# One 512 KB store at the end of a kernel, issued as eight transfers of 96, 11, 6, 5, 4, 3, 2 and 1 rows

## The chip, the cores and the metric

The kernel runs on one core of one Trainium2 chip. The metric is the device time of one execution in microseconds (us), lower being better; times given for a kernel are medians of several runs on the same chip.

## The reference

128 samples `x[b]` of 128 channels by 1024 steps (float32) each get the product of their own subject's 128 x 128 weight matrix added. There are eight subjects, and an index says which one each sample has.

```python
def reference(x, subjects, weights):        # x (128,128,1024), subjects (128,), weights (8,128,128)
    w = weights[subjects]
    return x + jnp.einsum('bct,bcd->bdt', x, w)
```

64 MiB are read and 64 MiB are written; one sample is 512 KB, 128 rows of 4 KB.

## The kernel before

The samples are worked on in tiles of four (`NT` = 32 tiles, index `i`). A tile lies in one of `SLOTS` = 12 buffers `xs[k]`, 128 partitions (rows) by four samples of 1024 float32, so a row of one sample is 4 KB in one partition. SyncE (SP) issues the loads, one for each sample, on its own queue (q1 in the profile): 48 at once, and from then on a tile's four whenever the stores out of its buffer have landed. The eight weight matrices are loaded once, into `w_all`.

The work runs over pairs of samples (`j` from 0 to 63; tile `i`, samples `q0` to `q1` of the tile). GpSimd copies each sample's matrix out of `w_all` into one of four small buffers (L196), TensorE multiplies into one of two PSUM buffers (L206), VectorE adds the product to `x` in place (L217) and counts up `s_added`. ScalarE (ACT) does no arithmetic. It waits for `s_added` and issues the stores on its own queue (q10 in the profile), through the helper `transfer` (L57):

- each pair of the first tile by itself (1 MB),
- each whole tile from then on (2 MB, after its second pair),
- and of the last tile: the first pair (1 MB, samples 124 and 125), then sample 126 by itself (512 KB, 128 rows), then, behind a barrier, sample 127 by itself (L231, called `last` here).

Both queues are served by the core's 16 DMA engines. A DMA counts its semaphore up by 16 (`DMA`) in all, and each engine's part of it ends with a small write to that semaphore. The records of the trace show a 128-row store of one sample as 128 packets of 4096 B and 16 such writes of 4 B: eight rows and one write for each engine.

At the end SP waits for the stores of the last twelve tiles, one semaphore after another (L229, L230), and the end of the program waits for `last`. The first critical section ends with a barrier between ACT and SP; it stands between ACT's issue of sample 126 and its issue of `last`. SP's waits at L229 and L230 come after that barrier, and ACT does not wait for them.

The line that decides how sample 126 is stored is the argument `q1 - (b == B - 1)` of L223: for the last pair it takes one sample off, so that one 512 KB store goes out. Its landing is counted on `s_pair[...][1]` of the last tile, for which the last turn of the loop at L228 waits.

Of the kernel before, what the change touches and what calls it, by code (L numbers as in the profile page):

```python
# [30 lines left out]
G = 2  # L31
H = 2
# [3 lines left out]
SLOTS = 12  # L36
# [5 lines left out]
DMA = 16  # L42

IDLE = 3

ROWS = 4
QUEUES = {mybir.EngineType.SP: "qSPDynamicHW", mybir.EngineType.Activation: "qActDynamicHW"}
# [2 lines left out]
def transfer(nc, engine, out, in_):  # L50

    later, nc._always_lower_symbolic_ap = nc._always_lower_symbolic_ap, False
    ins, outs = engine.lower_ap_dma(in_), engine.lower_ap_dma(out)
    nc._always_lower_symbolic_ap = later
    return engine.add_instruction(  # L57
        mybir.InstDMACopy(
            name=nc.get_next_instruction_name(),
            engine=engine.engine,  # L60
            ins=ins,
            outs=outs,
            mode="Copy",
            cce_op=ALU.bypass,
            queue=QUEUES[engine.engine],
        )
    )


@with_exitstack  # L70
def kernel(
    ctx: ExitStack,
    tc: tile.TileContext,
    x: bass.AP,
    subjects: bass.AP,
    weights: bass.AP,
    out: bass.AP,
):
    nc = tc.nc
    B, C, T = x.shape  # L80
    S, _, D = weights.shape
    NT = B // (G * H)

    def sbuf(name, *shape, dtype=F32):
        return ctx.enter_context(nc.sbuf_tensor(name, list(shape), dtype)).ap()

    given, near, wrap, index = (
        sbuf(name, 1, B, dtype=I32) for name in ("given", "near", "wrap", "index")
    )
    w_all = sbuf("w_all", C, S, D)  # L90
    ws = [sbuf(f"w{i}", C, 1, D) for i in range(W_SLOTS)]
    zeros = sbuf("zeros", C, N)
    xs = [sbuf(f"x{i}", C, H * G, T) for i in range(SLOTS)]
    ps = [
        ctx.enter_context(nc.psum_tensor(f"ps{i}", [D, G, T], F32)).ap() for i in range(P_SLOTS)
    ]

    s_given = tc.alloc_semaphore("s_given")
    s_wall = tc.alloc_semaphore("s_wall")
    s_index = tc.alloc_semaphore("s_index")  # L100
    s_zeros = tc.alloc_semaphore("s_zeros")
    s_copied = tc.alloc_semaphore("s_copied")
    s_product = tc.alloc_semaphore("s_product")
    s_added = tc.alloc_semaphore("s_added")

    s_pair = [[tc.alloc_semaphore(f"s_pair{i}_{h}") for h in range(H)] for i in range(SLOTS)]


    s_first = tc.alloc_semaphore("s_first")

    def emptied(i, h):

        turns = i // SLOTS
        return (DMA * G + (DMA if h == H - 1 else 0)) * turns

    def loaded(i, q):

        h = q // G
        return s_pair[i % SLOTS][h], emptied(i, h) + DMA * G

    def load(engine, i, q):
        k, h = i % SLOTS, q // G
        transfer(
            nc,
            engine,
            xs[k][:, q, :],
            x[i * H * G + q].rearrange("(a r) t -> a (r t)", r=ROWS),
        ).then_inc(s_pair[k][h], DMA)

    def store(i, q0, q1):  # L130
        k, b = i % SLOTS, i * H * G
        transfer(
            nc,
            nc.scalar,
            out[b + q0 : b + q1].rearrange("g d t -> d g t"),
            xs[k][:, q0:q1, :].rearrange("d (o g) t -> d o (g t)", g=min(G, q1 - q0)),
        ).then_inc(s_first if i == 0 and q1 == G else s_pair[k][(q1 - 1) // G], DMA)

    with tc.tile_critical():  # L139

        nc.scalar.dma_start(given, subjects.rearrange("(o b) -> o b", o=1)).then_inc(s_given, DMA)

        nc.vector.memset(zeros, 0.0).then_inc(s_zeros, 1)  # L143
        nc.tensor.wait_ge(s_zeros, 1)
        for _ in range(IDLE):
            nc.tensor.matmul(  # L146
                ps[P_SLOTS - 1][:, G - 1, :N], zeros[:, :D], zeros, start=True, stop=True
            )

        nc.vector.wait_ge(s_given, DMA)
        nc.vector.tensor_scalar(near, given, -S, S - 1, ALU.max, ALU.min).then_inc(s_index, 1)  # L153
        nc.vector.wait_ge(s_index, 1)
        nc.vector.tensor_scalar(wrap, near, 0, S, ALU.is_lt, ALU.mult).then_inc(s_index, 1)  # L155
        nc.vector.wait_ge(s_index, 2)
        nc.vector.tensor_tensor(index, near, wrap, ALU.add).then_inc(s_index, 1)  # L157
        nc.gpsimd.wait_ge(s_index, 3)


        nc.sync.dma_start(w_all, weights.rearrange("s c d -> c s d")).then_inc(s_wall, DMA)  # L161
        for i in range(NT):
            k = i % SLOTS
            if i == SLOTS:
                nc.sync.wait_ge(s_first, DMA)
            if i >= SLOTS:
                nc.sync.wait_ge(s_pair[k][H - 1], emptied(i, H - 1))
            for q in range(H * G):
                load(nc.sync, i, q)


        for j in range(NT * H):
            i, q0, q1 = j // H, j % H * G, (j % H + 1) * G
            k = i % SLOTS
            p = ps[j % P_SLOTS]

            ahead = j < P_SLOTS
            if ahead:  # L180
                nc.tensor.wait_ge(*loaded(i, q0))
            for q in range(q0, q1):
                b = i * H * G + q
                if b % R == 0:
                    _, subject = nc.values_load_multi_w_load_instructions(
                        index[0:1, b : b + R],
                        engines=[mybir.EngineType.Pool],
                        min_val=0,
                        max_val=S - 1,
                        skip_runtime_bounds_check_because="the index is clamped on the chip above",  # L190
                    )
                if b == 0:
                    nc.gpsimd.wait_ge(s_wall, DMA)
                if not ahead and q == q0:
                    nc.gpsimd.wait_ge(s_added, j - P_SLOTS + 1)
                copy = nc.gpsimd.tensor_copy(  # L196
                    ws[b % W_SLOTS], w_all[:, bass.ds(subject[b % R], 1), :]
                )
                if not ahead and q == q0:
                    copy.wait_op(*loaded(i, q0), "sem-ge")  # L200
            copy.then_inc(s_copied, 1)

            nc.tensor.wait_ge(s_copied, j + 1)
            for q in range(q0, q1):
                for t in range(0, T, N):
                    mm = nc.tensor.matmul(  # L206
                        p[:, q % G, t : t + N],
                        ws[(i * H * G + q) % W_SLOTS][:, 0, :],
                        xs[k][:, q, t : t + N],
                        start=True,  # L210
                        stop=True,
                    )
            mm.then_inc(s_product, 1)

            mine = xs[k][:, q0:q1, :]
            nc.vector.wait_ge(s_product, j + 1)
            nc.vector.tensor_tensor(  # L217
                mine, p, mine, ALU.add
            ).then_inc(s_added, 1)

            if i == 0 or q1 == H * G or i == NT - 1:
                nc.scalar.wait_ge(s_added, j + 1)
                store(i, q0 if i in (0, NT - 1) else 0, q1 - (b == B - 1))  # L223

    with tc.tile_critical() as waits:
        for i in range(NT - SLOTS, NT):  # L228
            nc.sync.wait_ge(s_pair[i % SLOTS][H - 1], emptied(i + SLOTS, H - 1))  # L229
        nc.sync.wait_ge(s_pair[(NT - 1) % SLOTS][0], emptied(NT - 1 + SLOTS, 0) + DMA)  # L230
    last = nc.scalar.dma_start(out[B - 1], xs[(NT - 1) % SLOTS][:, H * G - 1, :])  # L231

    tc.add_manual_dep(
        last.ins,
        waits.name,
        mybir.DependencyInfo(mybir.DependencyClass.NoSync, mybir.DependencyReason.SCHED_ONLY),
        reason="the end of the program waits for it",
    )
# [27 lines left out]
```

## Time and profile before

| what | value |
|---|---|
| device time, median of 3 runs | 326.48 us (326.29 to 326.70) |
| span of the profiled execution (first to last of the program's own instructions) | 325.4 us |
| median less that span | 1.1 us |
| TensorE / VectorE busy | 74% / 45% of the span |
| end of the last VectorE add | 278.7 us |
| DMA traffic | 134.85 MB, mean 414 GB/s |
| ACT begins to issue sample 126 | 300.46 us |
| ACT issues `last` | 305.02 us |
| the landings of `last` on its semaphore, first / median / last of 16 | 320.64 / 321.3 / 324.42 us |

The page has one profiled execution; the three runs are executions of the same program, and the profiled one has no device time of its own on the page, only its span. In what follows the 1.1 us that the median has over the span are taken as what lies around it. All times inside the execution count from the span's start. The DMA share of a stretch is the mean over 16 engines: 1.00 means that all were at work, 0.06 that one was. A row of the timeline that reads "ACTq" is the time for which ACT was held by issuing a DMA; the transfer itself goes on afterwards.

### The profile page before, as it was taken

What the parts mean: (1) busy time and instruction counts of PE and PEld (TensorE: products, weight loads), DVE (VectorE), ACT (ScalarE), POOL (GpSimd) and SP (SyncE); (2) the same over time, 40 slices, a digit from 0 to 9 for tenths busy, and PEclk for the clock granted to TensorE, in tenths of its full rate; (3) what the DMA queues carried; (4) which work ended last, traced back from release to release, by engine and by line L of the source; (5) the groups of instructions that cost most, each with busy time, mean ns of one, the idle gap of its engine ahead of it and who ended that gap; (6) DMA issues with size and microseconds to landing.
All of it is one profiled execution on the core that took longest, in us unless ns stands there. A gap on an engine that the chain in (4) does not pass through costs nothing.

```text
span 325.4 us, 1606 instructions
## 1 busy us (share of the span) xinstructions
PE 241.1 (74%) x518; PEld 95.2 (29%) x518; DVE 147.9 (45%) x68; POOL 34.3 (11%) x132
## 2 busy tenths in 40 slices
PE   6999988988888888888888888888888689000000
PEld 2444332333333333333333333333333233000000
DVE  1375754555555555454555555554554544200000
POOL 1011111011111111111011111111111010000000
PEclk9999999999999999999999999999999889655555
DMA  6999999999999999999999999999999999999994
GB/s 250 413 418 421 428 425 422 420 428 427 426 421 427 429 415 427 424 431 423 423 435 417 416 432 424 428 417 428 433 419 424 418 437 415 429 425 427 426 428 201
DMA packets 16074, 134.85 MB, mean 414 GB/s; under 512 B 2625, under 2 KB 3650, under 8 KB 3906
## 3 DMA queue, kind: packets, MB, share of 16 engines
q1 hardware_dynamic: 7184, 67.64, 49.7%
q10 hardware_dynamic: 8882, 67.11, 49.1%
q8 instruction: 4, 0.07, 0.1%
q14 instruction: 4, 0.03, 0.0%
HBM read 67.63 MB, written 67.11 MB: 414 GB/s over the span
## 4 chain that ended last, share of the span: by engine, by line
PE 42%; DVE 20%; issue 16%; POOL 4%; DMA 2%; POOLq 1%; SPq 0%
PE ps L206 42%; DVE x L217 20%; POOL w L196 4%; DMA x<-in_x_dram 2%; POOLq L196 1%; SPq L57 0%; SPq L161 0%; POOLq L139 0%; SPq L262 0%; SPq L139 0%
## 5 line engine op out<-in xcount | busy, mean ns | idle before, releaser
L206 PE MATMUL ps<-x,w 128*128 128x512 f32 x512 | 236.1, 607 | 33.6 <-POOL w L196 32.1
L217 DVE TENSOR_TENSOR x<-ps,x 128x2048 f32<-128x2048 f32 x64 | 146.7, 2292 | 129.1 <-PE ps L206 129.1
L206 PEld LDWEIGHTS ps<-x,w 128*128 128x128 f32 x512 | 93.3, 191 | 176.6 <-issue 93.9
L196 POOL COPY w<-w_all 128x128 f32 x128 | 34.1, 296 | 238.0 <-DMA x<-in_x_dram 207.7
L146 PE MATMUL ps<-zeros 128*128 128x512 f32 x6 | 5.0, 992 | 1.7 <-DVE zeros L143 1.7
L146 PEld LDWEIGHTS ps<-zeros 128*128 128x128 f32 x6 | 1.8, 328 | 3.7 <-issue 2.1
L143 DVE MEMSET zeros<- 128x512 f32 x1 | 0.5, 485 | 1.1 <-SPq L139 1.1
L153 DVE TENSOR_SCALAR near<-given 1x128 int32<-1x128 int32 x1 | 0.2, 215 | 0.6 <-DMA given<-in_itok_B_dram 0.6
L157 DVE CUSTOM_DVE_ANT_0 index<-near,wrap 1x256 uint16<-1x256 uint16 x1 | 0.3, 278 | 0.0
L155 DVE TENSOR_SCALAR wrap<-near 1x128 int32<-1x128 int32 x1 | 0.2, 216 | 0.0
L253 POOL MEMSET const-float32-0.0<- 128x1 f32 x1 | 0.1, 99 | 0.2 <-issue 0.2
L253 POOL MEMSET const-bfloat16-1.0<- 128x1 bf16 x1 | 0.1, 102 | 0.0
L253 POOL MEMSET const-uint8-127<- 128x1 uint8 x1 | 0.1, 102 | 0.0
L253 POOL MEMSET const-float32-1.0<- 128x1 f32 x1 | 0.1, 99 | 0.0
## 6 DMA issues: line engine op xcount, KB each, us to landing
x<-in_x_dram SPq DMA_DIRECT2D x128, 512.0 KB, 32.3
out_dram<-x ACTq DMA_DIRECT2D x30, 2048.0 KB, 47.3
out_dram<-x ACTq DMA_DIRECT2D x3, 1024.0 KB, 13.9
out_dram<-x ACTq DMA_DIRECT2D x2, 512.0 KB, 21.1
w_all<-in_L_cond_weights_dram SPq DMA_DIRECT2D x1, 512.0 KB, 4.5
given<-in_itok_B_dram ACTq DMA_DIRECT2D x1, 0.5 KB
```

The lines of the kernel that those rows point to most:

```text
L143: nc.vector.memset(zeros, 0.0).then_inc(s_zeros, 1)
L146: nc.tensor.matmul(ps[P_SLOTS - 1][:, G - 1, :N], zeros[:, :D], zeros, start=True, stop=True)
L153: nc.vector.tensor_scalar(near, given, -S, S - 1, ALU.max, ALU.min).then_inc(s_index, 1)
L155: nc.vector.tensor_scalar(wrap, near, 0, S, ALU.is_lt, ALU.mult).then_inc(s_index, 1)
L157: nc.vector.tensor_tensor(index, near, wrap, ALU.add).then_inc(s_index, 1)
L196: copy = nc.gpsimd.tensor_copy(ws[b % W_SLOTS], w_all[:, bass.ds(subject[b % R], 1), :])
L206: mm = nc.tensor.matmul(p[:, q % G, t : t + N], ws[(i * H * G + q) % W_SLOTS][:, 0, :], xs[k][:, q, t : t + N], start=True, stop=True,)
L217: nc.vector.tensor_tensor(mine, p, mine, ALU.add).then_inc(s_added, 1)
L253: nc = _bacc.Bacc("TRN2", target_bir_lowering=False, num_devices=1)
```

## The change

The store of sample 126 becomes eight stores, of rows 0 to 95, 96 to 106, 107 to 112, 113 to 117, 118 to 121, 122 to 124, 125 to 126, and 127. They are issued by ACT one after another, in this order and on the same queue, and count a semaphore of their own, `s_shares`, up to 128. The wait of SP for the last tile's second pair becomes a wait for `s_shares`. The store of samples 124 and 125 before it and `last` behind it are as they were.

```diff
+SHARES = 96, 11, 6, 5, 4, 3, 2, 1
...
+    s_shares = tc.alloc_semaphore("s_shares")
...
+    def store_rows(i, q, d0, d1):
+        return transfer(
+            nc,
+            nc.scalar,
+            out[i * H * G + q, d0:d1],
+            xs[i % SLOTS][d0:d1, q, :],
+        )
...
             if i == 0 or q1 == H * G or i == NT - 1:
                 nc.scalar.wait_ge(s_added, j + 1)
-                store(i, q0 if i in (0, NT - 1) else 0, q1 - (b == B - 1))
+                if b < B - 1:
+                    store(i, q0 if i in (0, NT - 1) else 0, q1)
+                else:
+                    d = 0
+                    for rows in SHARES:
+                        store_rows(i, q0, d, d + rows).then_inc(s_shares, DMA)
+                        d += rows
...
     with tc.tile_critical() as waits:
-        for i in range(NT - SLOTS, NT):
+        for i in range(NT - SLOTS, NT - 1):
             nc.sync.wait_ge(s_pair[i % SLOTS][H - 1], emptied(i + SLOTS, H - 1))
+        nc.sync.wait_ge(s_shares, DMA * len(SHARES))
         nc.sync.wait_ge(s_pair[(NT - 1) % SLOTS][0], emptied(NT - 1 + SLOTS, 0) + DMA)
     last = nc.scalar.dma_start(out[B - 1], xs[(NT - 1) % SLOTS][:, H * G - 1, :])
```

## The prediction, made before the change was run

> **What bounds the kernel now.** I read the page first: the row of DMA shares, the bytes under it and the two queues.
>
> ```profile
> DMA  6999999999999999999999999999999999999994
> GB/s 250 413 418 421 428 425 422 420 428 427 426 421 427 429 415 427 424 431 423 423 435 417 416 432 424 428 417 428 433 419 424 418 437 415 429 425 427 426 428 201
> ...
> q1 hardware_dynamic: 7184, 67.64, 49.7%
> q10 hardware_dynamic: 8882, 67.11, 49.1%
> ```
>
> The DMA engines are full from the second slice to the last but one, at 415 to 435 GB/s; only the first and the last slice (8.1 us each) fall off. The page's chain of waits follows TensorE and VectorE; the last add ends at 278.7 us, and the 47 us behind it are the stores' backlog. So the kernel is as long as its DMA traffic, and the change, which moves no byte more or less, can only act on the fall-off at the end. I therefore cut the end into short windows.
>
> ```profile
> core 0: us, PE busy (x) PEld busy (x) DVE busy (x) POOL busy (x), PEclk, DMA share, GB/s
> ...
> 319.50:320.00 0.50, 0.00 (x0) 0.00 (x0) 0.00 (x0) 0.00 (x0) 0.50 1.00 410
> 320.00:320.40 0.40, 0.00 (x0) 0.00 (x0) 0.00 (x0) 0.00 (x0) 0.50 0.95 389
> 320.40:320.80 0.40, 0.00 (x0) 0.00 (x0) 0.00 (x0) 0.00 (x0) 0.50 0.73 297
> 320.80:321.20 0.40, 0.00 (x0) 0.00 (x0) 0.00 (x0) 0.00 (x0) 0.50 0.50 205
> ...
> 321.60:322.00 0.40, 0.00 (x0) 0.00 (x0) 0.00 (x0) 0.00 (x0) 0.50 0.23 92
> 322.00:322.40 0.40, 0.00 (x0) 0.00 (x0) 0.00 (x0) 0.00 (x0) 0.50 0.05 20
> ...
> 323.60:324.00 0.40, 0.00 (x0) 0.00 (x0) 0.00 (x0) 0.00 (x0) 0.50 0.05 20
> 324.00:324.40 0.40, 0.00 (x0) 0.00 (x0) 0.00 (x0) 0.00 (x0) 0.50 0.00 0
> ```
>
> The last column but one is the share of 16 engines at work: all until 320, half at 321, and from 322.2 to 324.0 a share of 0.05 to 0.08, which is one engine. That one engine is the end of the kernel. The landing records of `last` say the same: counted from the first of the 16, nine engines are done within 0.75 us, six more between 1.39 and 1.91 us, and one at 3.78 us. I call it the late engine. It is late by the same 3.7 to 3.8 us at every store that lands after 271 us, so it only has to work off the queue that it has; which of the 16 it is, no record tells.
>
> Last, ACT's issues (start, time held) and SP's waits.
>
> ```profile
> 300.46 4.01 ACTq L57 DMA_DIRECT2D out_dram<-x  x1
> 305.02 0.54 ACTq L231 DMA_DIRECT2D out_dram<-x  x1
> ```
>
> ```profile
> SPq L139 <- ACTq L139: 26.1, 1, 26.1
> SPq L229 <- DMA out_dram<-x: 18.0, 3, 9.5
> ```
>
> ACT is held 4.01 us over sample 126, because the queue's rings are full, and 0.54 us over `last`, when there was room. Both are issued 13 us before the first engine comes to them.
>
> **The change part by part.** *What an engine pays for a row.* In the lone engine's stretch the eight 4096 B packets of `last` start 155 to 156 ns apart, and a semaphore write is followed 6 ns later by the next packet. With all engines at work the step is the same, so a row costs the engine that carries it 0.155 us, whatever the others do, and a further semaphore write 0.006 us.
>
> *Where the rows go.* Before, each engine has eight rows of sample 126. The load of the index, a single row, shows one data packet and one semaphore write by an engine: a transfer of one row occupies one engine. I take it (an assumption; the trace has no transfer of 2 to 15 rows) that 96 rows give six to each of 16 engines, and that a transfer of n rows below 16 gives one row each to n engines, counted from the same first engine every time. By place in that count the rows are 13, 12, 11, 10, 9, 8, five times 7 and five times 6, together 128. [...]
>
> *What that is worth.* If the late engine stands at place 12 to 16, it loses two rows: 2 x 0.155 = 0.31 us less. At places 7 to 11 it loses one and gets one more semaphore write: 0.15 less. At place 6: +0.01. At places 5, 4, 3, 2, 1: +0.17, +0.33, +0.50, +0.66 and +0.82 (five rows and seven writes). No other engine takes over the end: the next lands 1.87 us before the late one, and 0.82 more still leaves it 1.05 us ahead. So the most that the change can bring by its rows is 0.31 us, 0.1% of the time, and about 0.2% (0.65 us) is what a measurement of this kernel can tell from no change.
>
> *ACT.* One issue becomes eight. The first (six rows and a write for each engine instead of eight) is held by full rings as the one before, about 4 us. The other seven cost between 0.54 us (the issue of `last`) and 0.62 us (the longest of the first twelve, with room in the rings), 4.0 to 4.5 us together with the gaps; I take 4.2, as these rows are the same instruction. Behind them stand the barrier and `last`, which moves from 305.0 to about 309.3 us. The cover is the backlog: the first engine reaches sample 126 at 317.8 us, the late one at 321.5. So this costs nothing. Uncovered it would cost its 4.2 us.
>
> [...]
>
> *SP.* One wait changes its semaphore; nothing is queued behind it but the other waits of the end. In before, SP is through these 0.47 us ahead of the landing of `last`, and the shares land ahead of `last` on every engine as sample 126 did, so it stays hidden.
>
> *Sum.* The mean over places 6 to 16 is (0.01 - 5 x 0.15 - 5 x 0.31) / 11 = -0.21 us. On the profiled execution: span 325.4 - 0.2 = 325.2, with 1.1 around it 326.3, against a median of 326.48.
>
> [...]
>
> **The rivals.**
>
> *R1, the late engine is given more rows.* The place is sample 126's part of its ring; the price 0.17 to 0.82 us; it decides from place 5 down, and passes 0.65 us at places 2 and 1. For it: nothing in the trace ties lateness to a place, and five of 16 places have it. Against: 11 places do not. Time 326.7 to 327.3.
>
> *R2, ACT is held at each of the eight.* The 512 KB store was held 4.01 us and the 1 MB store before it 4.5, hardly less than 2 MB stores (4.7), so holding isn't in proportion to size. Eight times 4.0 would put `last` at some 333 us; the quickest landing of any of the helper's transfers took 5.2 us, so the end would come 13 us or more later: about 340. It decides from 2.6 us an issue (the 21 us to the late engine's arrival, divided by eight). Against it: `last` found room at once, and SP's queue held 15 to 16 transfers.
>
> *R3, the late engine is late by another amount.* Stores that land from 162 to 233 us show it 2.5 to 3.3 us behind, the one at 252 us 7.5, those after 271 us 3.7 to 3.8. The jump falls where the loads run thin. With other timing it may not come back the same: 0.5 to 1.2 us less, or as much more. Against: the three runs lie within 0.41 us. Time 325.3 to 326.0, seldom 327.
>
> *R4, the split isn't what it says.* If each small transfer goes to a single engine, that engine has 6 + 32 = 38 rows, 30 x 0.155 = 4.7 us more: 327.4 on one of the first engines (they are 3.78 us ahead), 331.2 on the late one. For it: the only small transfer of the trace used one engine. Against: it had only one row.
>
> **How the numbers follow.** Forecast (places 6 to 16): 0.48, all within 0.2%. R1: 0.25, of which 0.13 is within and 0.12 slower. R2: 0.05, slower. R3: 0.14, of which 0.12 faster, 0.02 slower. R4: 0.08, slower. Together faster 0.12, same 0.61, slower 0.27. The range is from 325.8 (the nearer half of R3) to 327.4 (the whole of R1 and measurement noise); outside lie R2, R4 and the far half of R3, under 0.2. The forecast's own range is 326.1 to 326.6.
>
> **What would show it.** In the profile of the changed kernel the packets of 4096 B stay 256 and the writes of 4 B on q10 become 561 - 16 + 48 = 593 (16+11+6+5+4+3+2+1 = 48). The landing counts of `s_shares` show the split. The last engine's packets between its last 8192 B packet and `last` number six, seven or eight if the forecast holds, nine to 13 under R1. Eight ACT issues stand between 300.5 and 309 us, seven of them near 0.6; holds of 4 us would be R2. Windows at the end should show one engine for about 1.5 to 1.9 us; a much shorter or longer stretch is R3. The forecast is wrong if the time leaves 326.1 to 326.6, and its mechanism if the late engine's rows don't fall.

## The result and the profile after

The changed kernel takes 328.17 us (median of 3, 328.05 to 328.42) against 326.48: 1.69 us more, ratio 1.0052, 95% interval 1.0032 to 1.0071. The forecast was 326.3, a little under the time before, in a range up to 327.4. The time is outside the range, and the kernel became slower where it was to become faster.

The page says that the body of the kernel is as it was; only the last two slices of the DMA rows have moved (before: 428 and 201 GB/s at the end).

```profile
DMA  7999999999999999999999999999999999999993
GB/s 253 414 418 427 428 420 427 423 424 425 426 430 423 426 424 425 419 428 429 426 424 422 424 427 423 426 427 425 425 424 423 428 423 427 425 429 425 429 422 144
DMA packets 16106, 134.85 MB, mean 413 GB/s; under 512 B 2657, under 2 KB 3682, under 8 KB 3938
```

The same bytes move in 32 packets more: the 48 - 16 semaphore writes that the prediction counted. The end in short windows:

```profile
320.00:320.40 0.40, 0.00 (x0) 0.00 (x0) 0.00 (x0) 0.00 (x0) 0.50 0.93 277
320.40:320.80 0.40, 0.00 (x0) 0.00 (x0) 0.00 (x0) 0.00 (x0) 0.50 0.51 205
320.80:321.20 0.40, 0.00 (x0) 0.00 (x0) 0.00 (x0) 0.00 (x0) 0.50 0.50 184
...
321.60:322.00 0.40, 0.00 (x0) 0.00 (x0) 0.00 (x0) 0.00 (x0) 0.50 0.45 133
322.00:322.40 0.40, 0.00 (x0) 0.00 (x0) 0.00 (x0) 0.00 (x0) 0.50 0.18 72
...
324.40:324.80 0.40, 0.00 (x0) 0.00 (x0) 0.00 (x0) 0.00 (x0) 0.50 0.07 31
324.80:325.20 0.40, 0.00 (x0) 0.00 (x0) 0.00 (x0) 0.00 (x0) 0.50 0.03 10
```

Read the last two columns together. Before, a share of 0.95 came with 389 GB/s and one of 0.50 with 205: 25.6 GB/s for each engine at work. After, 0.93 comes with 277 and 0.45 with 133, that is 18.5 GB/s an engine; the windows between them are less slow (0.51 with 205 is 25.1, 0.50 with 184 is 23.0). So in some windows the engines are not fewer, they are slower while at work: a busy share says that an engine has a packet in hand, not at what pace it moves. Then comes the stretch of one engine, now up to 325.

The packet records show where. In the kernel before, from 290 us on, none of the 256 packets of 4096 B (159 ns) and of the 8192 B ones (309 or 311 ns) is longer than that. After the change 21 are, by 5.35 us in all, and all of them start once the first engines have reached the eight transfers. The late engine's row packets of sample 126 take, in ns:

```
96-row transfer: 300, 295, 951, 380, 159, 159 | 11 rows: 159 | 6 rows: 159 | 5 rows: 159 | then eight of last, 159 each
```

ACT's issues, start and time held:

```profile
299.60 4.00 ACTq L59 DMA_DIRECT2D out_dram<-x  x1
...
303.63 0.94 ACTq L59 DMA_DIRECT2D out_dram<-x  x1
...
309.07 0.84 ACTq L59 DMA_DIRECT2D out_dram<-x  x1
...
310.56 0.39 ACTq L249 DMA_DIRECT2D out_dram<-x  x1
```

`last` is issued at 310.6 us and its first landing is at 320.6: the cover held.

**A measure of the end.** The landing records allow a finer measure than the time of a run. Stage A is the time from the last of the 16 landings of the last 2 MB store to the last landing of samples 124 and 125, B from there to the last landing of sample 126, C from there to that of `last`. In before it is 2.47, 1.23 and 1.26 us, 4.96 in all; after the change 2.68, 2.91 and 1.14, 6.73 in all, 1.77 us more, where the medians differ by 1.69. (The two spans differ by 1.0 only: the profiled execution of before was a long one, its landing of that 2 MB store 0.74 us later. Executions whose span and time are both known lie 1.7 to 1.85 us apart, so that span of 325.4 belongs to a time of about 327.1, not 326.5.) This sum follows the medians through all the kernels run, mostly within 0.2 us and at most 0.4, though it comes from one execution and they from several:

| kernel | how sample 126 is stored | A, B, C (us) | sum, less before | median less before (us) | ratio, 95% interval | packets too long, us in all |
|---|---|---|---|---|---|---|
| before | 128 rows | 2.47, 1.23, 1.26 | | | | 0, 0 |
| after | 96, 11, 6, 5, 4, 3, 2, 1 | 2.68, 2.91, 1.14 | +1.77 | +1.69 | 1.0052 (1.0032 to 1.0071) | 21, 5.35 |
| e1 | 96, 32 | 3.25, 1.30, 1.24 | +0.82 | +1.10 | 1.0034 (1.0021 to 1.0046) | 7, 1.50 |
| e2 | 8 x 128 rows of 512 B | 2.58, 1.59, 1.05 | +0.26 | +0.35 | 1.0012 (1.0003 to 1.0021) | 5, 0.05 |
| e3 | 8 x 16 rows | 3.74, 1.60, 0.98 | +1.35 | +1.33 | 1.0040 (1.0027 to 1.0053) | 27, 7.31 |
| e4 | as after, from DRAM | 2.87, 1.57, 1.14 | +0.61 | +0.58 | 1.0019 (1.0010 to 1.0028) | 4, 0.77 |
| e5 | 8 x 16, spread in DRAM | 3.85, 1.61, 0.96 | +1.45 | +1.84 | 1.0055 (1.0042 to 1.0068) | 26, 5.27 |
| e6 | 128 rows, 12 KB apart in DRAM | 2.46, 1.24, 1.26 | 0.00 | +0.13 | 1.0002 (0.9993 to 1.0011) | 0, 0 |
| e7 | 96, 8 x 4 | 3.99, 0.98, 1.25 | +1.25 | +1.28 | 1.0037 (1.0024 to 1.0050) | 37, 7.80 |
| e8 | 8 x 16, to scratch | 3.20, 1.76, 1.12 | +1.12 | +1.15 | 1.0036 (1.0023 to 1.0049) | 35, 6.63 |
| e9 | 16 from 0, 20, 64, 80, 96, 112 | 2.52, 1.18, 1.03 | -0.24 | -0.24 | 0.9991 (0.9982 to 0.9999) | 15, 2.51 |
| e10 | 16 from 16, 48, 64, 80, 96, 112 | 2.55, 1.18, 1.08 | -0.16 | -0.25 | 0.9995 (0.9985 to 1.0005) | 12, 3.11 |
| e11 | 16 from 0, 16, 48, 64, 80, 96, 112 | 3.66, 1.40, 0.99 | +1.09 | +1.34 | 1.0033 (1.0016 to 1.0050) | 21, 5.31 |
| e12 | 16 from 0, 32, 64, 80, 96, 112 | 2.55, 1.19, 1.01 | -0.22 | -0.18 | 0.9996 (0.9987 to 1.0004) | 18, 3.49 |
| e13 | rows 0 to 15, eight times | 2.54, 2.26, 1.28 | +1.11 | +1.10 | 1.0034 (1.0022 to 1.0046) | 89, 30.3 |
| e14 | rows 16 to 31, eight times | 3.58, 2.41, 1.28 | +2.32 | +2.36 | 1.0075 (1.0062 to 1.0089) | 115, 46.2 |
| e15 | rows 32 to 47, eight times | 2.53, 2.64, 1.23 | +1.44 | +1.32 | 1.0038 (1.0024 to 1.0052) | 104, 33.9 |
| e16 | rows 48 to 63, eight times | 4.09, 1.98, 1.23 | +2.34 | +2.53 | 1.0078 (1.0064 to 1.0092) | 116, 48.1 |
| e17 | e10 again | 2.94, 1.20, 1.04 | +0.21 | +0.27 | 1.0007 (0.9999 to 1.0016) | 14, 3.56 |
| e18 | e10 with 16 and 48 last | 3.19, 1.19, 1.04 | +0.46 | +0.50 | 1.0012 (1.0003 to 1.0021) | 12, 2.79 |

Stages are of one profiled execution each; medians are of 3 to 12 executions beside the kernel before on the same chip. "Too long" is over 165 ns for 4096 B and 317 ns for 8192 B.

### The profile page after: what moved, and what is told of

The parts are those of the page before. It is cut to its first block, busy times and chain, and to the rows that moved or that the text cites. A ratio compares the mean times of both kernels' runs of the same rounds, so it can differ in the third digit from the quotient of the medians.

```text
span 326.4 us, 1613 instructions
## 1 busy us (share of the span) xinstructions
PE 240.5 (74%) x518; PEld 95.3 (29%) x518; DVE 147.9 (45%) x68; POOL 34.3 (11%) x132
## 4 chain that ended last, share of the span: by engine, by line
PE 42%; DVE 20%; issue 16%; POOL 4%; DMA 2%; POOLq 1%; SPq 0%
PE ps L217 42%; DVE x L228 20%; POOL w L207 4%; DMA x<-in_x_dram 2%; POOLq L207 1%; SPq L59 0%; SPq L172 0%; POOLq L150 0%; SPq L280 0%; SPq L150 0%
```

## The experiments

### What lengthens the packets: e1 to e4

Three theories stood: A, the rows that an engine reads; B, the number of transfers and semaphore writes; C, nothing but the late engine's nine rows.

e1_96_32, the change without its seven small transfers:

```diff
-SHARES = 96, 11, 6, 5, 4, 3, 2, 1
+SHARES = 96, 32
```

> Sample 126 in two transfers, 96 and 32 rows (six and two rows for each of 16 engines): the change without its seven small transfers, rows even again. In the changed kernel the records show 21 packets of the end that take longer than in the kernel before (4096 B: 294 to 951 ns instead of 159), 5.35 us too much in all, 1.36 us of it on the late engine's part of the 96 rows. Theory A (which engine reads which partitions: in a 96-row transfer an engine reads six neighbouring rows, others than in a 128-row one, and gets into the way of engines that read the same partitions): long packets stay, 0.5 to 1.4 us over the kernel before. Theory B (the many small transfers and their semaphore writes make the packets long): no long packets, within 0.2 us of before. Theory C (only the number of rows of the late engine counts, nine in the changed kernel): no long packets, within 0.1 us of before.

Measured: +1.10 us with two transfers and eight rows for every engine. C and B fall: the rows are even, there is one transfer more than before, and still seven packets are too long; stage A alone is 0.78 us longer. How long the late engine is held in stage A differs much from profile to profile: with the same 96-row transfer first it takes 2.68 us in the changed kernel, 3.25 here and 3.99 in e7.

e2_cols, as many transfers as the change, but each of all 128 rows:

```diff
-SHARES = 96, 11, 6, 5, 4, 3, 2, 1
+SHARES = (128,) * 8
...
-            out[i * H * G + q, d0:d1],
-            xs[i % SLOTS][d0:d1, q, :],
+            out[i * H * G + q, :, d0:d1],
+            xs[i % SLOTS][:, q, d0:d1],
```

> Sample 126 in eight transfers of all 128 rows by 128 columns each (512 B a packet): as many transfers and more semaphore writes than the change, but every engine keeps the rows that it has in the kernel before. Theory A: no packets that wait; 0.1 to 0.4 us over before, for 64 packets of 512 B at 22 to 27 ns instead of eight at 155. Theory B: as the changed kernel or worse, 1.4 to 1.7 us over. Theory C: as A.

Measured: +0.35 us, and no packet more than 15 ns too long. B falls a second time. Stage B is 0.36 us longer, and smaller packets account for most of it: on the late engine packets of 512 B start 23.5 ns apart, so 64 of them and eight writes take 0.30 us more than eight of 4096 B and one write. Stages A and C differ by +0.11 and -0.21 us.

e3_8x16, even rows again, but 16 neighbours at a time:

```diff
-SHARES = 96, 11, 6, 5, 4, 3, 2, 1
+SHARES = (16,) * 8
```

> Sample 126 in eight transfers of 16 rows: one row for each engine in each, so eight rows for every engine as before, but all 16 engines read 16 neighbouring partitions at a time. Theory A: more and longer packets than in the changed kernel, over 5 us too much in all, and an end 1 to 3 us over before. Theory B: as the changed kernel, 1.4 to 1.7 us over, as there are as many transfers. Theory C: 0.04 us over before (seven more semaphore writes).

Measured: +1.33 us, 27 packets, 7.31 us. The prices of A are met. e2 has eight transfers too; it differs in the rows that a transfer reads, but also in the size of its packets. e13 to e16 below change the rows alone.

e4_dram, the change's split without reading SBUF:

```diff
-            xs[i % SLOTS][d0:d1, q, :],
+            x[i * H * G + q, d0:d1],
```

> The changed kernel, but the eight transfers of sample 126 take the input x of that sample in DRAM as their source instead of the sum in SBUF (this sample's product is left out of the output): the same split over engines, the same writes to DRAM, no reading of SBUF partitions. Theory A, with the collision on the side of SBUF: no long packets among the rest, and an end up to 0.3 us over before (the late engine's ninth row). With the collision on the side of the writes to DRAM: as the changed kernel, 1.4 to 1.7 us over. Theory B: as the changed kernel. A copy from DRAM to DRAM may have a pace of its own, which the late engine's rows would show when it is alone.

Measured: +0.58 us, 4 packets too long, 0.77 us; the late engine's nine rows take 159 ns each again. So most of the loss goes with the reading of SBUF. I had expected none, though: three 8192 B packets are held (392, 512 and 606 ns), and stage A is 0.40 us too long. What holds them when no transfer of sample 126 reads SBUF stays open.

### SBUF or DRAM: e5, e6, e8, and a place check, e7

e5_sbuf_only and its control e8_scratch write to a scratch tensor, 16 KB apart or row after row (e5 is shown; the comment, added here, has e8's line):

```diff
+    scratch = nc.dram_tensor("scratch", (512, T), F32).ap()
...
-SHARES = 96, 11, 6, 5, 4, 3, 2, 1
+SHARES = (16,) * 8
...
+        rows = scratch.rearrange("(g e r) t -> g e r t", e=16, r=4)
-            out[i * H * G + q, d0:d1],
+            rows[d0 // 16, :, 0],          # e8_scratch: scratch[d0:d1]
```

> [...] Theory A-SBUF (engines collide where they read the same partitions): long packets as in e3_8x16, some 7 us too much in all, and 0.8 to 1.9 us over before. Theory A-DRAM (they collide where they write to neighbouring places in DRAM): hardly any, within 0.3 us of before.

> The control of e5_sbuf_only: eight transfers of 16 rows, written to the scratch tensor row after row, as e3_8x16 writes them to the output (output of sample 126 left out). Both theories: as e3_8x16, 1.0 to 1.6 us over before, with some 7 us too much in long packets.

e6_dram_only keeps the 128-row store and spreads its rows in DRAM:

```diff
-SHARES = 96, 11, 6, 5, 4, 3, 2, 1
+SHARES = (128,)
...
+        rows = scratch[: 3 * 128].rearrange("(p r) t -> p r t", r=3)
-            out[i * H * G + q, d0:d1],
+            rows[:, 0],
```

> One transfer of 128 rows for sample 126, as in the kernel before on the side of SBUF, but written to a scratch tensor with its rows 12 KB apart, so that each engine writes to other places modulo 128 KB than it does elsewhere (output of sample 126 left out). A-SBUF: no long packets, within 0.2 us of before. A-DRAM: long packets, 0.5 us or more over before.

Measured: e5 +1.84 us with 26 packets too long, e8 +1.15 with 35, e6 +0.13 (its interval takes in no change) with none, and stages as in before to 0.01 us. Changing the places in DRAM made no long packet, changing the rows read in SBUF did: A on the side of SBUF. That e5 lies above e8, with fewer packets too long (5.27 us in all, where some 7 were expected), was not foreseen and stays open.

e7_96_4s:

```diff
-SHARES = 96, 11, 6, 5, 4, 3, 2, 1
+SHARES = (96,) + (4,) * 8
```

> The changed kernel with other shares: 96 rows and then eight transfers of four rows, so that four engines get 14 rows and the other twelve six. In the changed kernel the late engine had nine rows and four writes, which is place 5 of the count; here it should have six rows and one write, if its place is the engine's and not chance. Rows alone (theory C): 0.3 us under before. Theory A: the 96 rows collide as in e1_96_32, 0.5 to 1.1 us over before, and less than the changed kernel. Should the late engine have 14 rows, the place is not fixed.

Measured: the late engine has six rows and one write, as its place 5 in the changed kernel asks (any place from 5 on would do), so stage B is 0.98 us, 0.25 less than before, close to the 0.31 of two rows. But stage A is 3.99 us (three of the late engine's 8192 B packets took 555, 388 and 865 ns), and the whole +1.28 us. The saving by rows is real and is lost several times over.

### Whose rows: e9 to e18

The records name no row and no engine for a packet, so these runs vary the rows that are read. e9 to e18 store sample 126 in transfers of 16 rows from given first rows, some rows left out of the output or stored several times (e9 is shown, with a comment added here):

```diff
-SHARES = 96, 11, 6, 5, 4, 3, 2, 1
+SHARES = 0, 20, 64, 80, 96, 112        # e9; the first rows of the others are in the table
...
-                    d = 0
-                    for rows in SHARES:
-                        store_rows(i, q0, d, d + rows).then_inc(s_shares, DMA)
-                        d += rows
+                    for d in SHARES:
+                        store_rows(i, q0, d, d + 16).then_inc(s_shares, DMA)
```

> Which partitions must be read for the late engine to be held? Sample 126 in six transfers of 16 rows (0, 20, 64, 80, 96 and 112 onward; the other 32 rows of that sample are left out of the output), so six rows for each engine. [...] Time between 0.3 us under before (two rows less) and 0.7 us over (its own six rows collide). [...]

> [...]

Measured: both spare the late engine (A 2.52 and 2.55 us) and take the same time (326.50 and 326.49 us). That e10 would hold it was my expectation, and it failed. I formed another theory, eight neighbouring rows for each engine: 32 to 39 for the late one, which is called engine 4 below, its place 5 counted from zero:

> e9_spare and e10_touch left the late engine's part of the store before sample 126 at its pace (2.52 and 2.55 us from the last landing of the 2 MB store to the last landing of samples 124 and 125, against 2.47 in the kernel before and 3.20 to 3.85 with all eight transfers of 16 rows). Rows 36 to 47 are what both left out. Theory A8: a 128-row store gives an engine eight neighbouring rows, so engine 4 has rows 32 to 39, and it is held only by who reads those. Here seven transfers of 16 rows, all but rows 32 to 47 (left out of the output). A8: that stage stays under 2.6 us; time within 0.3 us of before, seven rows for the late engine. [...]

> Six transfers of 16 rows as in e9_spare and e10_touch, but these start at 0, 32, 64, 80, 96 and 112, so rows 32 to 47 are read and 16 to 31 and 48 to 63 are left out of the output. A8: the late engine is held, that stage takes 2.9 us or more, and the time is 0.4 us or more above e9_spare and e10_touch. [...]

Measured: e11 3.66 us, held; e12 2.55 us, spared. Both are the reverse of the eight-neighbour theory. Theory N, that six transfers of 16 rows are too few to hold the late engine and seven are not, fits all four; theory T has it held by seven or more, whatever they read. e13 to e16 decide it by reading one block of 16 rows eight times (e14 here):

```diff
-SHARES = 96, 11, 6, 5, 4, 3, 2, 1
+SHARES = (16,) * 8
...
-            xs[i % SLOTS][d0:d1, q, :],
+            xs[i % SLOTS][16 : 32, q, :],
```

> Eight transfers of 16 rows as in e3_8x16, but all eight read rows 0 to 15 of sample 126 and write them to the eight places (so the output of that sample is rows 0 to 15 eight times). Measured by the stage from the last landing of the 2 MB store to that of samples 124 and 125: 2.47 us before, 2.5 to 2.6 where the late engine was spared, 3.2 to 3.9 where it was held. [...] Theory T (no rows are its own; with seven or more such transfers it is held whatever they read): 3.0 us or more, 0.8 us or more over before.

> The same with rows 16 to 31 read eight times. [...] Eight neighbours: spared, under 2.7 us. Theory T: held.

> The same with rows 32 to 47 read eight times. [...] Eight neighbours: held, 3.0 us or more. Theory T: held.

> The same with rows 48 to 63 read eight times. [...] Eight neighbours: spared. Theory T: held.

Measured, stage A: rows 0 to 15 2.54 us, 16 to 31 3.58, 32 to 47 2.53, 48 to 63 4.09. The late engine is held in exactly the two that read rows 16 to 31 or 48 to 63, and its last 8192 B packets there, four in e14 and six in e16, take 568 to 608 ns, nearly twice their 311. With eight transfers each, e13 and e15 spare it: theories T and N fall. In e13 and e15 it is spared, and yet they lose 1.1 and 1.3 us: the other engines hold each other so long (30 and 34 us in all) that they end beside the late one. How hard 16 engines hold each other on 16 rows, the windows show; first a line of before, then e14, then e15:

```profile
319.00:320.00 1.00, 0.00 (x0) 0.00 (x0) 0.00 (x0) 0.00 (x0) 0.50 1.04 426
```

```profile
318.00:319.00 1.00, 0.00 (x0) 0.00 (x0) 0.00 (x0) 0.00 (x0) 0.50 1.13 336
319.00:320.00 1.00, 0.00 (x0) 0.00 (x0) 0.00 (x0) 0.00 (x0) 0.50 1.00 164
320.00:321.00 1.00, 0.00 (x0) 0.00 (x0) 0.00 (x0) 0.00 (x0) 0.50 1.08 139
321.00:322.00 1.00, 0.00 (x0) 0.00 (x0) 0.00 (x0) 0.00 (x0) 0.50 0.78 102
```

```profile
319.00:320.00 1.00, 0.00 (x0) 0.00 (x0) 0.00 (x0) 0.00 (x0) 0.50 0.93 217
320.00:321.00 1.00, 0.00 (x0) 0.00 (x0) 0.00 (x0) 0.00 (x0) 0.50 1.01 164
321.00:322.00 1.00, 0.00 (x0) 0.00 (x0) 0.00 (x0) 0.00 (x0) 0.50 0.91 127
```

All engines are busy at 139 to 164 GB/s, where the page of before shows 413 to 437 for the same share. The control e6, 128 rows with other places in DRAM, runs at full pace in the same stretch:

```profile
319.00:320.00 1.00, 0.00 (x0) 0.00 (x0) 0.00 (x0) 0.00 (x0) 0.50 1.00 410
320.00:321.00 1.00, 0.00 (x0) 0.00 (x0) 0.00 (x0) 0.00 (x0) 0.50 0.75 307
```

Theory A as first put, engines that read the same partitions, looks too narrow. The small transfers of the changed kernel, of 11 rows down to 1, count 32 semaphore writes for 32 rows, so an engine has one row of such a transfer; if that holds for 16 rows too, no two engines in one of them read the same row, and yet packets of 4096 B take up to 1278 ns there instead of 159. Blocks 32 rows apart do alike in stage A: 2.54 and 2.53 us in e13 and e15, 3.58 and 4.09 in e14 and e16. Why these two blocks hold the late engine is not shown: these kernels tell blocks of 16 rows apart, not single rows, and no record names the rows that an engine reads. That the two blocks have rows of its own in them is argued.

The exception is e10, which reads rows 16 to 31 and 48 to 63 once each and had 2.55 us. It was run again, to see whether that was one lucky profile, and with its order changed, the transfers from rows 16 and 48 last instead of first:

> e10_touch once more, unchanged (transfers of 16 rows from 16, 48, 64, 80, 96 and 112; the rest of sample 126 left out). [...]

> [...]

Measured: the very same kernel now has 2.94 us in stage A and +0.27 us in the median, and with rows 16 and 48 read last 3.19 us and +0.50 us. So this kernel holds the late engine in some executions and not in others, and e10's profile was of the shortest of its twelve (326.22 us, the longest 327.52). Yet e10's median was that of e9 on the same chip (326.49 and 326.50), so most of its executions lost little. That it is a matter of phase, whether other engines come to these two blocks just when the late engine reads there, is argued; e11 fits it, whose eight executions lie between 326.43 and 328.36. The order seems to count, but the two intervals (0.9999 to 1.0016 and 1.0003 to 1.0021) overlap, so that isn't shown.

e9 and e12, which spare the late engine and give it six rows instead of eight, take 0.24 and 0.18 us less than before (e12's interval takes in no change). As one and the same kernel gave -0.25 us in e10 and +0.27 in e17, beside the kernel before on two chips, differences of this size are not safe. They store only 96 of the 128 rows, so they are no faster version. I know of none: rows 16 to 31 and 48 to 63 must be read by someone, and where transfers of 16 rows read one of these blocks again and again, as in e14 and e16, the late engine's packets nearly double (568 to 608 ns for 311). That no split could gain was argued from this and not tried.

## Why the prediction was wrong, step by step

- **What bounds the kernel**: right. One engine is late, and the time is what this engine still has to do; stages A to C account for the time of every kernel here to 0.4 us.
- **Where the rows go**: the split is right, the forecast of the place is not. 593 writes of 4 B, 48 of them by the shares; the late engine has nine rows and four writes of sample 126, which is place 5, outside the forecast's places 6 to 16. It has nine rows in e4 too, and its six rows and one write in e7 fit that place.
- **What an engine pays for a row**: the step that failed. "A row costs the engine that carries it 0.155 us, whatever the others do" was read from packets of 128-row transfers alone (159 ns each, 155 to 156 apart). With other splits a row took up to 951 ns in the changed kernel, 1272 in e14 and 1278 in e16. In the late engine's part of the 96 rows the first four steps took 306, 301, 995 and 376 ns, 1.36 us more than four at 0.155. Which rows it read there, and which engines were in its way, no record tells. That reading SBUF is what held it is borne out by e4, where the same nine rows, taken from DRAM, cost 159 ns each.
- **R1**: the place was one of its five, at the price named: +0.17 us. It is a tenth of the loss, and alone it would have left the time at 326.65 us, inside the range. The sum: 0.17 for the ninth row, 1.36 in the first four rows, 0.21 in stage A, and about 0.15 from the last write of a store to its landing, against 0.12 less in stage C: 1.77 us. Why the landings took longer stays open.
- **ACT**: right in effect, the size off. The first issue was held 4.00 us as forecast; the other seven took 0.84 to 0.94 us, not 0.54 to 0.62, so `last` went out at 310.6 instead of 309.3, some 8 us before the first engine came to it. R2 did not happen. That full rings held the first issue is the prediction's reading; no record shows a ring. The profile before shows the holds: 0.56 to 0.62 us for ACT's first twelve stores, 1.9 to 14.5 us for the 22 behind them, sample 126 the last.
- **R3**: in part. The late engine was 3.09 us behind the first in the profile after and 3.72 in the one before, and the later landing in the profile before hid 0.7 us of the loss when spans alone are compared. In the profile before, the stores that land at 244 and 262 us were 4.7 and 6.3 us late as well, which the rival's list passes over.
- **R4**: did not happen.
- **The sum**: its 1.1 us around the span is in no run; where an execution has both a time and a span, they lie 1.7 to 1.85 us apart. The forecast of a difference does not rest on it.
- **The signs listed**: the counts of packets and writes came as said, and the nine rows said R1. The eight ACT issues stand there, but seven of them near 0.87 us, not 0.6, and the stretch of one engine is some 2.3 us (322.8 to 325.1), not 1.5 to 1.9, which the list would have put down to R3. Missing were the packet lengths, the one place where the loss is seen at once.

## What to carry to other kernels

A store that is cut by rows can cost more than the rows that it moves about: here 0.17 us for a row against 1.6 us for the rest, most of which goes with the reading of SBUF (+1.69 us with it, +0.58 in e4 without). If transfers have to be cut, cut them by columns and keep all 128 rows in each (e2 lost 0.35 us with eight transfers, e3 1.33). And look at bandwidth per busy engine in short windows, not at the busy share: a share of 1.04 stood beside 426 GB/s and one of 1.08 beside 139.

## What the hardware showed that was not expected

- A 4096 B packet of 159 ns takes up to 1278 ns, eight times as long, in e16, whose eight transfers all read rows 48 to 63; the late engine's 8192 B packets take nearly twice their 311 ns, 568 to 608 ns, where eight transfers read rows 16 to 31 or 48 to 63 (e14, e16).
- The DMA engine that is late has the same place, 5 of the prediction's count, in the kernels that tell it (after and e4 by nine rows; the six rows and one write in e7 agree). It is 3.0 to 4.0 us behind the first at the last 2 MB store in every profile. Why it falls behind was not studied.
- A transfer of 1 to 11 rows held ACT for 0.84 to 0.94 us, longer than the 0.39 us of the 128-row `last` behind it, in the same profile. `last` does not go through the helper, so the two are not the same call; but the helper's first 128-row stores were held 0.57 to 0.71 us there. Why the small ones take longer was not studied.
